# Attention with a null key and value: subtracting the null key, value and bias from the others

## The chip, the cores and the metric

The kernel runs on one core of a Trainium2 chip. The metric is the device time of one execution in microseconds (us). A core has five engines that run their own instruction streams in order and meet by semaphores: TensorE (PE; its weight loads are listed apart as PEld), VectorE (DVE), ScalarE (ACT), GpSimd (POOL) and SyncE (SP), which here issues nearly all transfers (DMAs).

## The reference

Multi-query attention with a null key, 64 sequences of 128 tokens, model width 512, 16 heads of width 64, one key and one value head for all of them. A layer norm comes before and after, and the input is added at the end.

```python
b, n, _ = x.shape                     # 64, 128
scale = DH ** (-0.5)
xn = layernorm(x, g_in)
q = (xn @ Wq).reshape(b, n, H, DH).transpose(0, 2, 1, 3) * scale
kv = xn @ Wkv
k, v = (kv[..., :DH], kv[..., DH:])
k = jnp.concatenate([nk, k], axis=1)  # nk = null_kv[0], the null key
v = jnp.concatenate([nv, v], axis=1)  # nv = null_kv[1], the null value
sim = jnp.einsum('bhid,bjd->bhij', q, k)
bias = jnp.concatenate([null_col, attn_bias], axis=-1)   # null_col: one number per head
sim = sim + bias
sim = jnp.where(causal_mask, neg, sim)
sim = jnp.where(mask_p[:, None, None, :], sim, neg)      # the null key is never masked
attn = jax.nn.softmax(sim, axis=-1)
out = jnp.einsum('bhij,bjd->bhid', attn, v)
out = out.transpose(0, 2, 1, 3).reshape(b, n, INNER) @ Wo
return x + layernorm(out, g_out)
```

Adding one number to all scores of a row leaves its softmax as it was. Since the weights of a row sum to one, the output is the null value plus the weighted sum of the values less the null value. Both kernels rest on the second fact; the second kernel also uses the first.

## The kernel before, in words

Everything is in 32-bit floats. A sequence is an item, four items are a group. One function, `step(n)`, runs from n = -6 to 62 and issues, in an order written out by hand, parts of the work of several items at once: statistics and normalisation of item n+10 or n+12, the token transposes, the query products of group (n+6)//4 (from the second group on by seven half-size products per block, `product`), keys and values of item n+6 (`kv_mm`, `kv_out`, `k_T`, `kT_out`), scores and softmax of items n+1 and n+2, weighted values of item n (`values`), and the output projection of items n-3 to n-1. All engines work through their streams in the order in which `step` wrote them.

**Keys, values and null scores.** `kv_mm` (L303) multiplies an item's 128 tokens by `wkv`, in four chunks of 128 rows of the model width; each call of the matmul is two PE instructions. `wkv` has 64 key columns, 64 value columns and 16 more, which give the null score of each head: the head's query weights times the null key, prepared before the steps by `weights_kv_prod` (POOL, a product over 1024 columns for each chunk) and `weights_kv` (VectorE: scaling, a reduction and `null_order`, two small copies). `kv_out` copies the keys twice side by side, and adds `vnb` to values and null scores: minus the null value, and the null biases. `nulls_move` (L326) puts the lower half of the keys' values, and the null scores of the heads that the other half of the partitions needs, into the tile `nv`, by two copies on ScalarE and two DMAs on SP, once for three items and once for one item in each group.

**Scores.** Partitions hold 64 query rows of two halves of the heads, and a row of the score tile S has a null column, 64 lower keys, 128 keys and a null column again, 194 in all, for 8 heads. On POOL, `bias_add` (L460) fills the 192 key columns with bias plus mask, and `null_copy` (L473) copies the null scores from `nv` to the two null columns. `scores_add` adds the matmul results, `scores_max` and `exps` (VectorE, ScalarE) go over keys with the null column, `scale` (POOL) multiplies the keys by one over the sum, `blocks_T` transposes 32x32 blocks on VectorE, and `blocks_move` sends them, by 14 DMAs on SP (L601), to the tile `aTb`, from which `value_mm` (L634) multiplies by the values.

**The start.** Loads are issued on SP in the order of the code: the first four items, `wq`, null key, `wkv`, then in `load_second` items 4 to 6, the second half of the biases (`load_bias(1)`), the mask, null bias and null value. A transfer into an item's buffer waits until PE has transposed the item before. `causal` (L195) masks the biases on POOL; `causal(1)` covers all partitions, so `load_bias(0)` comes after it. Between the steps -6 and -5, and -5 and -4, the code that prepares weights, mask values and bias stands; after step -5 come the statistics of item 6 and the three sums of query weights (`weight_sums`), and in step -4 the statistics of item 7.

```python
        if n == -6:
            for kc in range(1, KC):
                weights_kv_prod(kc)
            causal(1)
            load_bias(0)
            for kc in range(2):
                weights_kv(kc)
```

Of the kernel before, what the change touches and what calls it, by code (L numbers as in the profile page):

```python
# [17 lines left out]
def kernel(  # L18
# [70 lines left out]
    KVN = 2 * DH + H  # L89
# [60 lines left out]
    nkb = const.tile([P, DH], FP, name="nkb")  # L150
    nvb = const.tile([P, DH], FP, name="nvb")
    nv2 = const.tile([P, 1], FP, name="nv2")
    nbh = const.tile([P, H], FP, name="nbh")
    biasp = const.tile([P, R8, NL + N], FP, name="biasp")
# [13 lines left out]
    for kc in (3, 1):  # L168
        nc.sync.dma_start(out=wq[:, kc, :], in_=wq_r[:, kc, :])
    nc.sync.dma_start(out=nkb, in_=cond[0].partition_broadcast(P))  # L170
    nc.sync.dma_start(
        out=wkv[:, :, 0 : 2 * DH], in_=w_kv.rearrange("(kc p) f -> p kc f", p=P)
    )

    def load_second():
        for m in (4, 5, 6):
            load_x(m)
        load_bias(1)
        load_mask(0)
        nc.sync.dma_start(out=nbh, in_=null_bias.partition_broadcast(P))  # L180
        nc.sync.dma_start(out=nvb, in_=cond[1].partition_broadcast(P))
        for r in range(2):
            nc.sync.dma_start(
                out=nv2[r * DH : (r + 1) * DH, :], in_=cond[1].unsqueeze(1)
            )

    def load_bias(u):
        rows = slice(u * DH, (u + 1) * DH)
        bias_r = attn_bias.rearrange("(u f r) i j -> u r i f j", u=2, r=2)[u]
        for r in range(2):  # L190
            rf = slice(r * NF, (r + 1) * NF)
            nc.sync.dma_start(out=biasp[rows, rf, 0:NL], in_=bias_r[r, 0:DH, :, 0:NL])
            nc.sync.dma_start(out=biasp[rows, rf, NL:], in_=bias_r[r, DH:N])

    def causal(u):  # L195

        rows = slice(0, P if u else DH)
        for keys, base in ((slice(0, NL), -DH * u), (slice(NL, NL + N), DH - DH * u)):
# [9 lines left out]

    def load_late():
# [7 lines left out]
    nc.gpsimd.memset(biasp[0:DH], 0.0)  # L217

# [7 lines left out]
    vnb = const.tile([P, DH + H], FP, name="vnb")  # L226
# [7 lines left out]
    xT, qT, kT, vs, nv, mneg = {}, {}, {}, {}, {}, {}  # L234
# [66 lines left out]
    ktok = {}  # L301

# [13 lines left out]

    def kv_out(m, pkv):
        g, t = divmod(m, GB)
        k = bp.tile([P, 2, DH], FP, tag="ktok", name=f"ktok_{m}")
        nc.vector.tensor_copy(k, pkv[:, 0:DH].unsqueeze(1).broadcast_to([P, 2, DH]))  # L320
        ktok[m] = k
        if t == 0:
            vs[g] = hp.tile([P, GB, DH + H], FP, tag="vs", name=f"vs_{g}", bufs=3)
        nc.vector.tensor_tensor(vs[g][:, t, :], pkv[:, DH:], vnb, ALU.add)

    def nulls_move(g, ts):  # L326

        if ts.start == 0:
            nv[g] = hp.tile([P, GB, DH + H], FP, tag="nv", name=f"nv_{g}")
        lo, hi = slice(0, DH), slice(DH, P)  # L330
        n1, n0 = slice(DH, DH + R8), slice(DH + R8, DH + H)
        nc.scalar.copy(nv[g][lo, ts, n1], vs[g][lo, ts, n0])
        nc.scalar.copy(nv[g][hi, ts, n0], vs[g][hi, ts, n1])
        nc.sync.dma_start(
            out=nv[g][hi, ts, 0 : DH + R8], in_=vs[g][lo, ts, 0 : DH + R8]
        )
        nc.sync.dma_start(out=nv[g][lo, ts, n0], in_=vs[g][hi, ts, n0])
# [110 lines left out]
    def mask_neg(g):  # L448
        mneg[g] = gp.tile([P, GB, NL + N], FP, tag="mneg", name=f"mneg_{g}", bufs=1)
        m8 = m8s.pop(g).rearrange("p (t j) -> p t j", t=GB)  # L450
        for keys, m in ((slice(0, NL), m8[:, :, 0:NL]), (slice(NL, NL + N), m8)):
            nc.vector.tensor_scalar(
                mneg[g][:, :, keys], m, 0.0, NEG, ALU.is_equal, ALU.mult
# [6 lines left out]
    def bias_add(b):  # L460
# [3 lines left out]
        else:  # L464
            S[b] = sp.tile([P, R8, ROW], FP, tag="s", name=f"s_{b}")
        nc.gpsimd.tensor_tensor(  # L466
            S[b][:, :, 1 : ROW - 1],
            biasp,
            mneg[g][:, t].unsqueeze(1).broadcast_to([P, R8, NL + N]),
            ALU.add,  # L470
        )

    def null_copy(b):  # L473
        g, t = divmod(b, GB)
        nc.gpsimd.tensor_copy(
            S[b][:, :, 0 : ROW : ROW - 1],
            nv[g][:, t, DH:].rearrange("p (k e) -> p e k", k=2),
        )

# [154 lines left out]
    def value_mm(b, u, half, keys, vals, slots, start=True):  # L634
        for r in range(2):
            nc.tensor.matmul(  # L636
                pos[b][u][r * DH : (r + 1) * DH, half],
                vals[keys, b % GB, 0:DH],
# [8 lines left out]
    def values(b, split):  # L647
# [6 lines left out]
        g = b // GB  # L654
# [5 lines left out]
        value_mm(b, 0, 0, lo, vs[g], slice(0, 2))  # L660
        value_mm(b, 1, 0, hi, nv[g], slice(0, 2))
        if split:
            value_mm(b, 0, 1, lo, vs[g], slice(2, 4))
            value_mm(b, 1, 1, hi, vs[g], slice(4, 6))
# [4 lines left out]
        else:  # L669
            value_mm(b, 0, 1, slice(0, P), vs[g], slice(2, 4))  # L670
            value_mm(b, 1, 1, slice(0, P), vs[g], slice(4, 6))

    def values_end(b, split):
        g = b // GB
        if split:
            value_mm(b, 1, 1, lo, vs[g], slice(4, 6), start=False)
            value_mm(b, 0, 1, hi, vs[g], slice(2, 4), start=False)
# [174 lines left out]
    prods = {}  # L852

    def null_order(out, heads):

        for u in range(2):
            nc.vector.tensor_copy(
                out[:, (1 - u) * R8 : (2 - u) * R8].rearrange("p (r f) -> p r f", r=2),
                heads[:, u * R8 : (u + 1) * R8].rearrange("p (f r) -> p r f", r=2),
            )  # L860

    def weights_kv_prod(kc):

        pool, tag = ((sp, "s"), (sp, "s"), (hp, "sb"), (hp, "xb"))[kc]
        bufs = None if kc < 2 else 1
        prods[kc] = pool.tile([P, H, DH], FP, tag=tag, name=f"prod_{kc}", bufs=bufs)
        nc.gpsimd.tensor_tensor(
            prods[kc],
            wq[:, kc, :].rearrange("p (h d) -> p h d", d=DH),
            nkb.unsqueeze(1).broadcast_to([P, H, DH]),  # L870
            ALU.mult,
        )

    def weights_kv(kc):
        nc.vector.tensor_scalar(
            wkv[:, kc, 0 : 2 * DH], wkv[:, kc, 0 : 2 * DH], gin[:, kc : kc + 1], None, ALU.mult
        )
# [436 lines left out]
```

## Time and profile before

| what | before |
|---|---|
| three timed runs | 1120.65, 1121.5, 1123.69 us (median 1121.5) |
| span of the profiled execution | 1117.9 us |
| around the span: median less span | 3.6 us |
| PE, DVE, ACT, POOL busy in the span | 1088.6, 808.8, 676.5, 743.0 us |
| pk matmuls (L308), 128x144 | 488 of 286 ns |
| null copies (L475) | 64 of 205 ns |
| bias_add (L466) | 64 of 3455 ns |
| ktok copies (L320), 128 columns | 61 of 280 ns |
| vs additions (L324), 80 columns | 61 of 231 ns |
| copies of nulls on ACT (L332, L333) | 64 of 186 to 208 ns |

The page gives the span, from the first to the last instruction; of the whole profiled execution it gives no other time. A line of the profile names the source line, the engine, the operation, the tile written and the tiles read, the shape and the count; behind a bar stand the total busy time and the mean of one in ns, then the idle time of the engine just before and what ended it. In an order of time the columns are start and length in us. [...]

### The profile page before, as it was taken

How to read it: one execution, taken by the hardware profiler on the slowest of the kernel's cores; microseconds unless marked ns; L12 is line 12 of the kernel's file. 1: busy time of each engine (PE TensorE's matmuls, PEld its weight loads, DVE VectorE, ACT ScalarE, POOL GpSimd, SP SyncE). 2: the span in 40 equal slices, each digit the busy share in tenths (PEclk: the TensorE clock that was granted, in tenths of full speed). 3: DMA queues.
4: the chain of work that ended last, by engine and by line, in shares of the span. 5: the costliest groups of instructions: out<-in, count | busy, mean ns of one | idle time of the engine just before them, and what ended most of it. 6: DMA issues, size and time to landing. Idle time of an engine off the chain costs nothing.

```text
span 1117.9 us, 27535 instructions
## 1 busy us (share of the span) xinstructions
PE 1088.6 (97%) x9794; PEld 875.1 (78%) x9794; DVE 808.8 (72%) x1743; ACT 676.5 (61%) x2709; POOL 743.0 (66%) x587
## 2 busy tenths in 40 slices
PE   8899999999999999999999999999999999999987
PEld 6576788888888788888888888888888888888633
DVE  6576578777768767777877877877776786666862
ACT  2365577565667566667656667756666765657651
POOL 6446967577676667758566676757767675677832
PEclk9999999999999999999999999999999999999999
DMA  5323244443634534354343534444353453422333
GB/s 189 125 70 71 79 137 125 128 118 91 169 97 126 132 108 131 101 149 113 128 127 89 159 100 138 124 128 119 93 168 99 125 133 114 106 68 76 98 106 99
DMA packets 107864, 130.09 MB, mean 116 GB/s; under 512 B 29264, under 2 KB 72528, under 8 KB 105936
## 3 DMA queue, kind: packets, MB, share of 16 engines
q1 hardware_dynamic: 106480, 126.96, 40.1%
q8 instruction: 78, 1.28, 0.5%
q10 hardware_dynamic: 1248, 1.38, 0.4%
q14 instruction: 58, 0.48, 0.1%
HBM read 54.86 MB, written 31.46 MB: 77 GB/s over the span
## 4 chain that ended last, share of the span: by engine, by line
PE 70%; DVE 7%; DMA 7%; SPq 6%; POOL 4%; issue 3%; ACT 3%; POOLq 0%; DVEq 0%; ACTq 0%
PE pa L422 15%; PE pyX L750 14%; PE pyY L750 7%; PE ps L495 7%; PE po L636 7%; PE pc L422 7%; DMA x<-in_x_dram 6%; SPq L601 4%; PE pk L308 4%; PE pw L422 3%; PE pyw L750 3%; PE py L697 2%; ACT s L522 2%; POOL s L466 1%; SPq L295 1%
## 5 line engine op out<-in xcount | busy, mean ns | idle before, releaser
L522 ACT ACTIVATE s<-s,nmax 128x65 f32<-128x65 f32 (+1 forms) x1024 | 372.0, 368 | 0.4
L466 POOL TENSOR_TENSOR s<-biasp,mneg 128x1536 f32<-128x1536 f32 x64 | 221.1, 3455 | 101.4 <-DVE sb L575 98.2
L543 POOL TENSOR_TENSOR s<-s,rinv 128x512 f32<-128x512 f32 (+1 forms) x128 | 189.3, 1479 | 122.8 <-DVE nmro L794 89.8
L680 ACT ACTIVATE oT<-po,nv 128x512 f32<-128x512 f32 x128 | 80.9, 683 | 200.1 <-PE po L636 198.8
L522 ACT ACTIVATION_READ_ACCUMULATOR s<-s,nmax 128x1 f32 x1024 | 194.7, 190 | 0.0
L750 PE MATMUL pyX<-wT,oT 128*128 128x256 f32 x696 | 164.8, 380 | 0.5 <-DVE kyu L762 0.5
L750 PEld LDWEIGHTS pyX<-wT,oT 128*128 128x128 f32 x696 | 131.8, 190 | 19.7 <-DVE kyu L762 0.9
L495 PEld LDWEIGHTS ps<-kT,qT 64*64 64x64 f32 x4096 | 94.2, 133 | 45.4 <-DVE s L508 23.1
L508 DVE TENSOR_TENSOR s<-ps,s 128x512 f32<-128x512 f32 (+1 forms) x128 | 121.5, 949 | 8.1 <-PE ps L495 6.6
L422 PE MATMUL pa<-xS,wq 128*128 128x256 f32 x480 | 123.5, 380 | 1.0 <-ACT ku L433 1.0
L495 PE MATMUL ps<-kT,qT 64*64 64x64 f32 (+1 forms) x4096 | 118.0, 249 | 3.6 <-DVE s L508 2.7
L513 DVE TENSOR_REDUCE nmax<-s 128x8 f32<-128x520 f32 (+1 forms) x128 | 120.1, 939 | 1.5
L575 DVE STREAM_TRANSPOSE sb<-s 128x1536 f32<-128x1536 f32 x62 | 110.0, 1774 | 13.4 <-POOL s L543 6.5
L636 PE MATMUL po<-aTb,vs 64*64 64x256 f32 (+1 forms) x1240 | 119.1, 378 | 0.0
L433 ACT COPY ku<-pa 128x256 f32<-128x256 f32 x120 | 44.6, 372 | 88.4 <-PE pa L422 88.2
L422 PEld LDWEIGHTS pa<-xS,wq 128*128 128x128 f32 x480 | 86.7, 190 | 11.2 <-ACT ku L433 1.8
L308 PE MATMUL pk<-wkv,xT 128*128 128x144 f32 x488 | 69.9, 286 | 0.0
L422 PE MATMUL pa<-xS,wS 128*128 128x256 f32 x240 | 67.8, 405 | 0.0
L443 DVE TENSOR_TENSOR qT<-pw,kp 128x256 f32<-128x256 f32 x60 | 25.4, 424 | 56.9 <-ACT kp L433 56.9
L636 PEld LDWEIGHTS po<-aTb,vs 64*64 64x64 f32 (+1 forms) x1240 | 57.4, 133 | 10.2 <-issue 3.8
L308 PEld LDWEIGHTS pk<-wkv,xT 128*128 128x128 f32 x488 | 63.4, 191 | 0.1
L804 ACT ACTIVATE yn<-y,nmro,rstdo 128x512 f32<-128x512 f32 x58 | 45.3, 782 | 29.2 <-DVE nmro L794 29.2
(120 smaller groups left out, 2096.3 us busy)
## 6 DMA issues: line engine op xcount, KB each, us to landing
aTb<-sb SPq DMA_DIRECT2D x369, 64.0 KB
x<-in_x_dram SPq DMA_DIRECT2D x64, 256.0 KB
res<-in_x_dram SPq DMA_DIRECT2D x64, 256.0 KB
out_dram<-y SPq DMA_DIRECT2D x64, 256.0 KB
aTb<-sb SPq DMA_DIRECT2D x492, 32.0 KB
xd<-xb SPq DMA_DIRECT2D x14, 1024.0 KB
xT<-xd SPq DMA_DIRECT2D x56, 256.0 KB
wo<-in_L_cond_Wo_dram SPq DMA_DIRECT2D x1, 2048.0 KB
```

The lines of the kernel that those rows point to most:

```text
L308: nc.tensor.matmul(pkv, xT[g][:, t, kc, :], wkv[:, kc, :], start=(kc == 0), stop=(kc == KC - 1),)
L422: nc.tensor.matmul(prod[tag], w[:, kc, f * P : (f + 1) * P], t[:, :, kc, :], start=(start and kc == 0), stop=(kc == HK - 1), skip_group_ch ...
L466: nc.gpsimd.tensor_tensor(S[b][:, :, 1 : ROW - 1], biasp, mneg[g][:, t].unsqueeze(1).broadcast_to([P, R8, NL + N]), ALU.add,)
L495: nc.tensor.matmul(pv[u * DH : (u + 1) * DH, r, f, :], qT[g][rows, f, t, hf, u], kT[b][rows, 0:nk], start=True, stop=True,)
L508: nc.vector.tensor_tensor(sv, pss.pop((b, hf)), sv, ALU.add)
L513: nc.vector.tensor_reduce(nmax[b][:, hf], S[b][:, :, WITH_NULL[hf]], AX.X, ALU.max, negate=True)
L522: nc.scalar.activation(row, row, AF.Exp, bias=nmax[b][:, hf, k : k + 1], accum_out=rsum[b][:, hf, k : k + 1],)
L543: nc.gpsimd.tensor_tensor(sv, sv, rinvs.pop((b, hf)).unsqueeze(2).broadcast_to([P, R8, sv.shape[2]]), ALU.mult,)
L575: nc.vector.transpose(sb.rearrange("p j e q -> p e j q"), S[b][:, :, 1 : ROW - 1].rearrange("p e (j k) -> p e j k", k=Q),)
L636: nc.tensor.matmul(pos[b][u][r * DH : (r + 1) * DH, half], vals[keys, b % GB, 0:DH], aT_of(b)[keys, slots, r * NF : (r + 1) * NF], start=s ...
L680: nc.scalar.activation(oT[b][:, u * NF : (u + 1) * NF, :].rearrange("p f (s q) -> p s f q", q=Q), po[u].rearrange("p h i f q -> p (h i) f q"),
L750: nc.tensor.matmul(prod[key], h[:, c, :], w[:, c, :], start=(start and c == 0), stop=(c == HC - 1), skip_group_check=not start,)
```

## The change

Null key, null value and null bias are subtracted from the keys, the values and the biases; then the null score is zero for every row, and no column is computed, moved or copied for it.

- `wkv` keeps its 128 columns. The products, reductions and reordering that filled the other 16 go, and `weights_kv` is one multiplication over all four chunks.
- `kv_out` subtracts the null key and the null value, broadcast to all partitions in `nkv`, from keys and values.
- `nulls_move` becomes `values_move`, which is one DMA; the two ScalarE copies and the second DMA go.
- Bias and mask tiles get the null columns of S, filled once with zero, and `bias_add` covers all 194 columns of a row; `null_copy` goes. The mask tile is one fixed tile.
- `null_shift` subtracts each head's null bias from the biases on VectorE, after `causal(1)` and after `causal(0)`.

```diff
-    KVN = 2 * DH + H
+    KVN = 2 * DH
...
-    biasp = const.tile([P, R8, NL + N], FP, name="biasp")
+    biasp = const.tile([P, R8, ROW], FP, name="biasp")
...
-    nc.sync.dma_start(out=nkb, in_=cond[0].partition_broadcast(P))
-    nc.sync.dma_start(
-        out=wkv[:, :, 0 : 2 * DH], in_=w_kv.rearrange("(kc p) f -> p kc f", p=P)
-    )
+    nc.sync.dma_start(out=wkv, in_=w_kv.rearrange("(kc p) f -> p kc f", p=P))
...
+    def null_shift(u):
+
+        rows = slice(u * DH, (u + 1) * DH)
+        nc.vector.tensor_copy(
+            nbp[rows].rearrange("p (r f) -> p r f", r=2),
+            nbh[rows, u * R8 : (u + 1) * R8].rearrange("p (f r) -> p r f", r=2),
+        )
+        nc.vector.tensor_tensor(
+            biasp[rows, :, 1 : ROW - 1],
+            biasp[rows, :, 1 : ROW - 1],
+            nbp[rows].unsqueeze(2).broadcast_to([DH, R8, NL + N]),
+            ALU.subtract,
+        )
...
+    nc.gpsimd.memset(biasp[DH:, :, 0 : ROW : ROW - 1], 0.0)
...
+    nc.gpsimd.memset(mneg[:, :, 0 : ROW : ROW - 1], 0.0)
...
-        nc.vector.tensor_copy(k, pkv[:, 0:DH].unsqueeze(1).broadcast_to([P, 2, DH]))
+        nc.vector.tensor_tensor(
+            k,
+            pkv[:, 0:DH].unsqueeze(1).broadcast_to([P, 2, DH]),
+            nkv[:, 0:DH].unsqueeze(1).broadcast_to([P, 2, DH]),
+            ALU.subtract,
+        )
...
-        nc.vector.tensor_tensor(vs[g][:, t, :], pkv[:, DH:], vnb, ALU.add)
+        nc.vector.tensor_tensor(vs[g][:, t, :], pkv[:, DH:], nkv[:, DH:], ALU.subtract)
...
-        nc.scalar.copy(nv[g][lo, ts, n1], vs[g][lo, ts, n0])
-        nc.scalar.copy(nv[g][hi, ts, n0], vs[g][hi, ts, n1])
-        nc.sync.dma_start(
-            out=nv[g][hi, ts, 0 : DH + R8], in_=vs[g][lo, ts, 0 : DH + R8]
-        )
-        nc.sync.dma_start(out=nv[g][lo, ts, n0], in_=vs[g][hi, ts, n0])
+        nc.sync.dma_start(out=nv[g][hi, ts], in_=vs[g][lo, ts])
...
         nc.gpsimd.tensor_tensor(
-            S[b][:, :, 1 : ROW - 1],
+            S[b],
             biasp,
-            mneg[g][:, t].unsqueeze(1).broadcast_to([P, R8, NL + N]),
+            mneg[:, t].unsqueeze(1).broadcast_to([P, R8, ROW]),
             ALU.add,
         )
-
-    def null_copy(b):
...
-    def weights_kv(kc):
-        nc.vector.tensor_scalar(
-            wkv[:, kc, 0 : 2 * DH], wkv[:, kc, 0 : 2 * DH], gin[:, kc : kc + 1], None, ALU.mult
-        )
-        nq = small.tile([P, H], FP, tag="nq", name=f"nq_{kc}")
-        nc.vector.tensor_reduce(nq, prods.pop(kc), AX.X, ALU.add)
-        null_order(wkv[:, kc, 2 * DH :], nq)
+    def weights_kv():
+        nc.vector.tensor_tensor(
+            wkv, wkv, gin.unsqueeze(2).broadcast_to([P, KC, KVN]), ALU.mult
+        )
...
         if n == -6:
-            for kc in range(1, KC):
-                weights_kv_prod(kc)
             causal(1)
+            null_shift(1)
             load_bias(0)
-            for kc in range(2):
-                weights_kv(kc)
+            weights_kv()
         if n == -5:
-            for kc in range(2, KC):
-                weights_kv(kc)
             causal(0)
+            null_shift(0)
             mask_neg(0)
-            nc.vector.tensor_scalar(vnb[:, 0:DH], nvb, -1.0, None, ALU.mult)
-            null_order(vnb[:, DH:], nbh)
```

## The prediction

> **What bounds the kernel now.** I read the page first (busy shares, then the chain that ended last), then the busy time by stage, then the groups with shapes kept apart, then the order of time in the first 50 us and in one steady stretch on SyncE's queue.
>
> ```profile
> span 1117.9 us, 27535 instructions
> ...
> PE 1088.6 (97%) x9794; PEld 875.1 (78%) x9794; DVE 808.8 (72%) x1743; ACT 676.5 (61%) x2709; POOL 743.0 (66%) x587
> ...
> PE 70%; DVE 7%; DMA 7%; SPq 6%; POOL 4%; issue 3%; ACT 3%; POOLq 0%; DVEq 0%; ACTq 0%
> ```
>
> TensorE (PE) carries 70% of the chain; no other engine has 8%. By stage (columns: PE, weight load, DVE, ACT, POOL, granted clock, DMA share, GB/s):
>
> ```profile
> 20.00:46.00 26.00, 21.36 (x74) 12.14 (x73) 18.17 (x41) 6.58 (x11) 15.79 (x11) 0.93 0.41 125
> ...
> 100.00:130.00 30.00, 27.74 (x268) 21.90 (x261) 19.12 (x42) 19.82 (x83) 26.85 (x22) 1.00 0.24 62
> ...
> 330.00:530.00 200.00, 198.49 (x1842) 166.28 (x1841) 151.22 (x330) 127.68 (x511) 137.39 (x109) 1.00 0.44 123
> ```
>
> From 130 to 1040 us PE is busy over 99% (198.49 of 200 here), so a microsecond of its stream is about a microsecond of the span. Only before 130 us and after 1040 us does something else end waits. Two places matter. In 20 to 46 us PE idles 4.6 us and the clock falls to 0.93; the matmuls (PE) and the engines they wait for, in order of time (start, length, what):
>
> ```profile
> 36.00 0.60 PE L268 MATMUL pxT<-ident,x 128*128 128x128 f32 x4
> 36.43 1.15 PE L308 MATMUL pkv<-wkv,xT 128*128 128x144 f32 x8
> 41.44 2.19 PE L308 MATMUL pkv<-wkv,xT 128*128 128x144 f32 x8 [3.86 <-ACT xT L269]
> ...
> 44.25 1.58 PE L308 MATMUL pkv<-wkv,xT 128*128 128x144 f32 x8 [0.41 <-DVE vs L324]
> ...
> 32.02 0.69 DVE L241 BATCH_NORM_STATS2 st<-x 128x6 f32<-128x512 f32 x1
> ...
> 30.08 1.08 POOL L199 TENSOR_SCALAR_AFFINE_SELECT biasp<-biasp 64x1024 f32<-64x1024 f32 x1 [0.44 <-DMA biasp<-in_fside_16xSxS_dram]
> ```
>
> The 3.86 us is VectorE's lateness: statistics of x_6 at 32.02, three weight sums, statistics of x_7, then ScalarE's normalisation of x_7 at 39.61, and behind that in ScalarE's order the eviction of xT which pkv waits for. The second place is SyncE's queue at the start of every fourth step:
>
> ```profile
> 365.41 0.61 SPq L120 DMA_DIRECT2D x<-in_x_dram  x1
> 366.13 0.69 SPq L334 DMA_DIRECT2D nv<-vs  x1
> 366.86 0.64 SPq L337 DMA_DIRECT2D nv<-vs  x1
> 369.88 11.27 SPq L601 DMA_DIRECT2D aTb<-sb  x14
> ...
> SPq L601 <- DMA x<-in_x_dram: 18.0, 17, 2.1
> ```
>
> A train of 14 attention-block moves mostly takes 9.0 to 10.5 us (9.05 at 353.78); behind an x load with a late landing it takes 11.27 to 11.87, and there PE stalls at po: I count 0.59, 0.83, 1.46, 0.64, 0.41 and 0.67 us from the matmul starts, 4.6 us in all. In the built program the eight hardware DMA semaphores go round, so each transfer waits for the one eight places ahead.
>
> **The change, part by part.** Profiled span 1117.9; the timed median is 1121.5, so 3.6 us lie around the span, which I keep.
>
> 1. *K/V projection, 144 to 128 columns.* 488 pk matmuls are in this group:
>
> ```profile
> L308 PE MATMUL pk<-wkv,xT 128*128 128x144 f32 x488 | 69.9, 286 | 0.0
> ...
> 12.99 0.83 PE L1214 MATMUL busy<-ident 128*128 128x128 f32 x6
> ```
>
> A row of eight takes 1.15 us with 0.286 for the last, so starts are (1.15-0.286)/7 = 123 ns apart. For 128 columns, with a 128x128 weight load each, there are two rows: four transposes start at 36.00 and the next matmul at 36.43, 108 ns apart; six "busy" matmuls take 0.83 us with 0.275 for one, 111 ns apart. I take 110.5: 12.5 ns x 488 = **-6.1 us** (ends 12 and 15 ns: -5.9 and -7.3). The 24 pkv are in the startup stall and count there. [...]
>
> 2. *Queue places.* Two value moves become one (32 DMAs and about 0.6 us of issue each leave SyncE's queue). In the step above x now stands one place nearer the train, so the train's seventh move, not its sixth, waits for x, and one issue (11.27/14 = 0.8 with the wait, 0.6 without) no longer lies behind the landing. Of six stalls of 4.6 us, 0.6 x 6 = 3.6 at most goes (0.41 and 0.59 cannot give more than themselves); but their length is set off PE, so a PE that does two K/V groups less 0.1 us each grows them by 0.2 x 6 = 1.2. I take **-2.0** (ends 0.0 and -3.4; +1.2 if the place brings nothing). Next late is the following move's landing.
>
> 3. *Startup, VectorE and POOL.* Out go four POOL products (9.8 us), four reductions (4.8), four scalings (5.2) and ten small copies and one scaling (3.0). In come one scaling of 512 columns (0.7, as L809's 692 ns for that size), two copies (0.17 each) and two bias subtractions of 64x1536 (1.8 each: L387's 1.22 for 1024 and L575's 1774 ns for 1536). But the subtraction waits for the masked bias, and in VectorE's order it stands ahead of the mask, the statistics of x_6, the weight sums and the statistics of x_7. POOL, without products, masks the first half on landing (about 17.5 to 19 instead of 23.98); the loads of the second half no longer wait for it but for the x load ahead of them on SyncE (issued 21.47, held by PE's transposes), so they start at 21.84 instead of 24.67 and end 3.2 us earlier. The mask of 30.08 moves to 26.9, ends at 28.0, the subtraction ends at 29.8, mask values (0.55), statistics of x_6 at 30.35 instead of 32.02: **-1.65 us** of the 3.86 (the wait of DVE itself, about 4 us, costs nothing else: what stands behind it is counted here). Ends: loads land as late as before, then 30.08+1.08+1.8+0.55 = 33.5 against 32.02, +1.5; all of the wait goes, -3.9. I take -1.65 by the issue rows. One row warns: a wkv scaling took 2.23 us while POOL multiplied and 0.28 while it waited. At both subtractions POOL's next work waits for VectorE, so I charge nothing; if it bit, +2 us. [...] Two more memsets run at 1.3 to 5.6 us, where POOL idles 2.96; one broadcast load less at 4.66 lets wkv's load start earlier, while x_4 still waits for PE.
>
> 4. *Clock.* The two groups of eight after the stall take 2.19 and 1.58 us against 1.15 at full clock: 1.04 + 0.43 = 1.47 us of slow clock. The stage's 0.93 goes with a 3.86 us gap; gaps of 1.02 and 0.45 near 10 us left the clock at 1.00. Shrunk to 2.2 the gap lies between; ends 0 and -1.47, I take **-1.0**, nearer the short gaps. [...]
>
> 5. *POOL around 100 to 130 us*, where it is 26.85 of 30 busy and released PE's pyY at 125.24. Two of 64 null copies (13.1 us in all, 205 ns each) lie there: -0.4; bias_add grows from 1536 to 1552 columns, 3455 x 16/1536 = 36 ns, twice. **-0.35** (ends 0, -0.6). The other copies, and 27.5 us in which POOL waited for the value move, are covered by PE: POOL is 66% busy; likewise bias_add's 2.3 us more.
>
> 6. *K minus null key* costs VectorE nothing: copying 128 columns is 280 ns; a PSUM+SBUF subtraction is 231 for 80 columns and 416 for 256, so (416-231)/176 x 48 + 231 = 281. Values go from 80 to 64 columns, -17 ns. 64 ScalarE copies (12.6 us in all) are under PE's cover; without it at most one 0.4 us pair a step.
>
> Sum: -6.1 -2.0 -1.65 -1.0 -0.35 = -11.1; span 1106.8, with the 3.6 around it **1110.5 us**.
>
> **Rivals.**
> - *The startup gives nothing*: bias lands late, the subtraction (a new wait on VectorE) holds x_6 as long as the reductions did, +1.5, and the clock still drops. For it: the in-order wait, rows of 256 and 512 bytes at the same DMA rates. Against: 2.8 us earlier issue. -6.1-2.0-0.35+1.5 = 1114.5.
> - *Narrower matmuls don't pay*: loads of weights (191 ns each by their row) hold the spacing at 123. Against: 108 and 111 ns above. Then -5.0: 1116.5.
> - *PE's gain is given back*: the four-step cycle is a loop through x landing (9.6 us), SyncE and VectorE, and all 16 cycles, not six, pull even. 0.2 x 16 = 3.2 back, no queue gain, no startup gain: 1121.5-6.1+3.2-0.35+1.5 = 1119.8, within the noise.
> - *VectorE becomes the bound (slower)*: the key subtraction reads PSUM and a stride-0 SBUF operand and pays POOL's interference of 2 us (2.23-0.28) in each of 61 steps. VectorE has 16.4-12.4 = 4 us free a step, but kT, ktok and vs stand ahead of x's statistics, whose chain ends in the PE stalls. It decides once it costs over 0.18 us a step on that path (61 x 0.18 = 11). At 2 us in the 16 x-bound steps: +32-11 = 1142. Against: 231 ns for vs, of the same operand kinds beside a working POOL.
> - That the arithmetic is not removed can be left out: in the built program no instruction on null columns but the wider bias_add is left.
>
> **How the numbers follow.** Chances: forecast 0.66 (own range 1106 to 1113.5), startup nothing 0.14, narrow matmul 0.07, given back 0.07, slower 0.06. The measurement tells about 0.3%, 3.4 us: faster means under 1118.1. The first three cases are faster (0.87), given back is same (0.07), the last slower (0.06). The low end takes -7.3-3.4-3.9-1.47-0.6 = -16.7 reduced to 1106, since not all ends come together; the high end takes in the narrow-matmul case: 1117.
>
> **What would show it.** L308's spacing near 110 ns and its group's mean near 272; trains behind the x load about 0.6 us shorter and fewer po stalls; PE's wait before the second pkv near 2.2 us and 20 to 46 us at clock 1.00; ktok at 281 ns; POOL without its wait on nv. Wrong would be: ktok or the subtraction far above 0.3 and 1.8 us, a second pkv later than 41.4 us, or po stalls in most cycles.

## The result, and the profile after

The changed kernel takes 1106.85 us in the median of four runs (1106.42 to 1110.19); the kernel before took 1121.97 us beside it. The ratio is 0.988, with a 95% interval of 0.986 to 0.990: 1.2% faster. The prediction was 1110.5 us.

In the profiled execution, which took 1106.42 us, the span is 1104.5 us, so 1.9 us lie around the span (1.7 to 2.2 in all executions, of either kernel and of every experiment). The prediction kept 3.6 us there, which mixed the span of one execution with the median of others. Of the span itself 13.4 us went.

The page of the changed kernel, span, busy time and chain by engine:

```profile
span 1104.5 us, 27326 instructions
...
PE 1081.3 (98%) x9794; PEld 868.1 (79%) x9794; DVE 795.7 (72%) x1729; ACT 665.5 (60%) x2645; POOL 706.0 (64%) x521
...
PE 81%; DVE 5%; DMA 4%; ACT 4%; SPq 3%; POOL 2%; issue 1%; DVEq 0%; POOLq 0%; ACTq 0%
```

PE's share of the chain rose from 70% to 81%, DMA and SyncE's queue fell from 13% to 7%. The busy times by stage (columns: PE, weight load, DVE, ACT, POOL, granted clock, DMA share, GB/s):

```profile
20.00:46.00 26.00, 24.14 (x84) 12.79 (x83) 15.87 (x37) 6.92 (x12) 10.07 (x8) 1.00 0.39 113
100.00:130.00 30.00, 28.50 (x209) 23.09 (x208) 18.77 (x41) 18.63 (x80) 27.00 (x19) 1.00 0.31 78
330.00:530.00 200.00, 199.54 (x1857) 166.86 (x1856) 153.25 (x335) 126.84 (x506) 134.54 (x97) 1.00 0.44 122
```

PE idles 1.9 us from 20 to 46 us (4.6 before) and 0.46 us from 330 to 530 us (1.51 before). Both programs issue the same 9794 matmuls in the same order, so the start of matmul number k in the two traces says where the time went:

| matmul | before | after | gained so far |
|---|---|---|---|
| 400 | 75.75 | 72.64 | 3.1 |
| 1200 | 162.54 | 158.20 | 4.3 |
| 7200 | 812.42 | 801.05 | 11.4 |
| 8400 | 943.08 | 930.08 | 13.0 |
| last | 1111.69 | 1098.28 | 13.4 |

So in these two executions 3.1 us come from the startup, 1.2 from there to 160 us, 8.7 from the steady stage, 0.4 from the end. One execution is a coarse measure of a stage: from matmul 1200 to 8400 this one took 771.9 us, and that of an experiment below that changes only the startup (*The statistics of x_6 ahead of the subtraction*) took 775.8. A difference between two steady stages is good to about 4 us.

The groups that answer to those shown of before:

```profile
L321 PE MATMUL pk<-wkv,xT 128*128 128x128 f32 x488 | 64.5, 275 | 0.0
...
L335 DVE TENSOR_TENSOR ktok<-pk,nkv 128x128 f32<-128x128 f32 x61 | 17.1, 280 | 0.0
...
L479 POOL TENSOR_TENSOR s<-biasp,mneg 128x1552 f32<-128x1552 f32 x64 | 205.3, 3208 | 112.0 <-DVE sb L580 108.8
```

A row of eight pk matmuls now takes 1.06 us with 0.275 for the last, so starts are 112 ns apart against 123: each starts before the one ahead of it has ended, and in a row one costs the spacing. The key subtraction takes the 280 ns of the old copy. bias_add covers 16 columns more and takes 247 ns less, which the prediction did not expect. In order of time, SyncE's queue ahead of a train of the changed kernel:

```profile
423.54 0.62 SPq L120 DMA_DIRECT2D x<-in_x_dram  x1
424.26 0.53 SPq L351 DMA_DIRECT2D nv<-vs  x1
427.91 10.31 SPq L606 DMA_DIRECT2D aTb<-sb  x14
```

And from its waits (us in total, times, longest), SyncE's for x and PE's for the moved blocks:

```profile
SPq L606 <- DMA x<-in_x_dram: 9.6, 11, 1.5
...
PE po L641 <- DMA aTb<-sb: 1.3, 1, 1.3
```

The trains behind the four xT loads take 10.49 us in the mean of the twelve between 130 and 930 us (9.77 to 11.10) against 11.22; behind anything else the means are 9.3 to 9.6 in both kernels. SyncE waits 9.6 us for x in 11 moves, not 18.0 us in 17. PE waits 1.3 us for moved blocks, not 4.3, but 3.0 of the 4.3 and all of the 1.3 lie after 1040 us; for the steady stage the matmul starts say more. Counted from them, between 130 and 930 us, the six gaps at po of 0.41 to 1.46 us (4.6 in all) are gone, and three of 0.17 to 0.29 (0.65 in all) are left. Four of 0.34 to 0.39 have come up at ps, the scores, where PE waits for VectorE and not for a move (three of the four in one line, with lengths from the modelled ends of 130 to 930 us):

```profile
PE ps L500 <- DVE done L673: 0.7, 3, 0.2
```

The startup of the changed kernel, PE and VectorE in order of time:

```profile
37.40 1.06 PE L321 MATMUL pkv<-wkv,xT 128*128 128x128 f32 x8
40.00 1.13 PE L321 MATMUL pkv<-wkv,xT 128*128 128x128 f32 x8 [1.55 <-DVE vs L344]
41.44 0.33 PE L356 MATMUL pkT<-ident,ktok 128*128 128x128 f32 x1 [0.31 <-ACT xT L284]
41.73 1.13 PE L321 MATMUL pkv<-wkv,xT 128*128 128x128 f32 x8
42.70 0.27 PE L356 MATMUL pkT<-ident,ktok 128*128 128x128 f32 x1
42.81 1.45 PE L387 MATMUL pq<-xT,wq 128*128 128x512 f32 x3
...
29.81 1.75 DVE L215 TENSOR_TENSOR biasp<-biasp,nbp 64x1536 f32<-64x1536 f32 x1 [4.20 <-POOL biasp L198]
31.48 0.61 DVE L465 TENSOR_SCALAR mneg<-m 128x256 f32<-128x256 uint8 x2
32.02 0.68 DVE L256 BATCH_NORM_STATS2 st<-x 128x6 f32<-128x512 f32 x1
```

In this execution the statistics of x_6 start at 32.02, exactly as before. Yet the second pkv starts at 40.00 instead of 41.44, because it now waits for VectorE's vs and not for ScalarE's eviction of xT (40.80 to 41.39 in both profiles): as built, it writes the PSUM buffer that the first pkv left, not the one that the transposes left. The eviction now delays only the later pkT, by 0.31 us, and the groups after it run at 1.13 us, at full clock.

The start at 32.02 belongs to this execution, in which the clock was halved from 11.93 to 15.34 us. Four experiments below keep the startup order of the changed kernel (the width undone, the value move split by partitions, POOL's wait, bias_add in rows), and in their profiles the clock is full there. The statistics of x_6 then start at 29.98 to 30.39 us and the second pkv at 37.96 to 38.38. From the one with the split move, VectorE and PE:

```profile
28.07 1.75 DVE L215 TENSOR_TENSOR biasp<-biasp,nbp 64x1536 f32<-64x1536 f32 x1 [2.96 <-POOL biasp L198]
...
30.28 0.68 DVE L256 BATCH_NORM_STATS2 st<-x 128x6 f32<-128x512 f32 x1
...
38.26 1.13 PE L321 MATMUL pkv<-wkv,xT 128*128 128x128 f32 x8 [1.33 <-DVE vs L344]
```

### The profile page after: what moved, and what is told of

It reads as the page before. It is cut to its first block, busy times and chain, and to the rows that moved or that the text cites. A ratio compares the mean times of both kernels' runs of the same rounds, so it can differ in the third digit from the quotient of the medians.

```text
span 1104.5 us, 27326 instructions
## 1 busy us (share of the span) xinstructions
PE 1081.3 (98%) x9794; PEld 868.1 (79%) x9794; DVE 795.7 (72%) x1729; ACT 665.5 (60%) x2645; POOL 706.0 (64%) x521
## 4 chain that ended last, share of the span: by engine, by line
PE 81%; DVE 5%; DMA 4%; ACT 4%; SPq 3%; POOL 2%; issue 1%; DVEq 0%; POOLq 0%; ACTq 0%
PE pa L436 17%; PE pyX L755 16%; PE pc L436 8%; PE pyY L755 8%; PE ps L500 8%; PE po L641 7%; PE pk L321 4%; PE pw L436 4%; PE pyw L755 4%; DMA x<-in_x_dram 3%; PE py L702 3%; ACT s L527 2%; SPq L606 2%; PE pq L387 1%; DVE s L513 1%
## 5 line engine op out<-in xcount | busy, mean ns | idle before, releaser
L479 POOL TENSOR_TENSOR s<-biasp,mneg 128x1552 f32<-128x1552 f32 x64 | 205.3, 3208 | 112.0 <-DVE sb L580 108.8
L641 PE MATMUL po<-aTb,vs 64*64 64x256 f32 (+1 forms) x1240 | 115.3, 379 | 0.0
L261 POOL TENSOR_TENSOR rstd<-rstd,nhalf 128x1 f32<-128x1 f32 x64 | 35.7, 558 | 60.4 <-DVE rstd L260 55.4
L321 PE MATMUL pk<-wkv,xT 128*128 128x128 f32 x488 | 64.5, 275 | 0.0
```

Source lines behind the costliest of these rows:

```text
L321: nc.tensor.matmul(pkv, xT[g][:, t, kc, :], wkv[:, kc, :], start=(kc == 0), stop=(kc == KC - 1),)
L479: nc.gpsimd.tensor_tensor(S[b], biasp, mneg[:, t].unsqueeze(1).broadcast_to([P, R8, ROW]), ALU.add,)
L641: nc.tensor.matmul(pos[b][u][r * DH : (r + 1) * DH, half], vals[keys], aT_of(b)[keys, slots, r * NF : (r + 1) * NF], start=start, stop=Tru ...
```

## The experiments

All times stand beside runs of the kernel before on the same chip. A ratio is to that kernel; differences between two experiments are good to about 3 us, as their intervals say.

### The width alone, undone and done

The changed kernel with the old width (16 columns of zeros):

```diff
-    KVN = 2 * DH
+    KVN = 2 * DH + H
...
+    nc.gpsimd.memset(wkv[:, :, 2 * DH :], 0.0)
```

> The changed kernel with the K/V projection 144 columns wide again (16 zero columns in the weights, results not used), nothing else. My theory: the pk matmuls start 123 ns apart again instead of 112, 488 x 11.5 ns = 5.6 us more, 1106.9 -> 1112.5 us, nearly all of it between 130 and 1030 us. Rival (the gain came from POOL and SyncE, the projection's width was covered): no more than 1 us, below 1108.

Measured: 1109.62 us, ratio 0.9894 (0.9876 to 0.9912). That is 2.8 us more than the changed kernel by the medians, 1.6 with 3.1 either way by the ratios, where the longer spacing alone is 488 x 11 ns = 5.4 us. Its pk matmuls stand 123 ns apart again (69.9 us in the group, as before the change), but SyncE waits less for x than in the changed kernel, and the gaps at po and ps, 2.2 us in sum there, are 0.6 us here:

```profile
SPq L609 <- DMA x<-in_x_dram: 5.8, 11, 1.0
```

That fits a loop in which a slower PE gives x more time to land.

The other direction, the kernel before with its projection narrowed. It leaves out the products of the queries with the null key. All else is kept but for VectorE: the addition of the values is narrowed too, and a copy per group puts in the null biases.

```diff
-                pkv,
+                pkv[:, 0 : 2 * DH],
...
-                wkv[:, kc, :],
+                wkv[:, kc, 0 : 2 * DH],
...
+            nc.vector.tensor_copy(
+                vs[g][:, :, DH:], vnb[:, DH:].unsqueeze(1).broadcast_to([P, GB, H])
+            )
```

> The kernel before with the K/V projection narrowed to 128 columns and nothing else changed: the 16 null columns of the moving tile are not multiplied (this leaves out the products of the queries with the null key: the null scores hold only the null bias), all copies, both null moves and every wait stay. Theory (PE and SyncE's train share the four-step cycle, so part of what PE saves comes back as longer po stalls, as the widened kernel showed with 2.8 us of 5.6): spacing 111 ns, the K/V part 5.4 us shorter, the po stalls longer than the 4.6 us of before, in all 2 to 3.5 us faster than before, about 1119. Rival of the prediction's sum (every nanosecond of PE's stream counts): 5.4 to 6.1 us faster, about 1116.3. Rival that the cycle is wholly SyncE's: no change, 1122.

Measured: 1118.85 us, ratio 0.9965 (0.9953 to 0.9978): 3.3 us by the medians, 2.5 to 5.3 by the ratio. The waits of this kernel (in total, times, longest):

```profile
SPq L606 <- DMA x<-in_x_dram: 21.0, 17, 2.6
...
PE po L641 <- DMA aTb<-sb: 6.0, 6, 1.7
```

Before they were 18.0 us and 4.3 us; the trains behind the x load grew from 11.22 to 11.41, and the gaps at po between 130 and 930 us from 4.6 to 6.5. So about 2 us of the 5.4 came back as longer waits, with spacing at 112 ns as it should be. That PE's own loop alone lengthened them is not shown, since this run also has the copies on VectorE:

```profile
L324 DVE COPY vs<-vnb 128x64 f32<-128x64 f32 x16 | 9.3, 580 | 0.0
```

The changed kernel has no such copies, and there the width is worth at most 4.7 us by the ratios. Both runs say that the narrowing pays less than its own length, neither by much more than its uncertainty.

### The queue place alone, undone and done

First the changed kernel with its value move split by columns into two:

```diff
-        nc.sync.dma_start(out=nv[g][hi, ts], in_=vs[g][lo, ts])
+        for c in (slice(0, 48), slice(48, DH)):
+            nc.sync.dma_start(out=nv[g][hi, ts, c], in_=vs[g][lo, ts, c])
```

> The changed kernel with each move of the values split into two DMAs of 48 and 16 columns, so that SyncE's queue has as many transfers as before. My theory: in the step behind each x load the train's sixth move waits for x again, those trains take 11.3 us and more instead of 10.2 to 10.8, and the po stalls come back: 2 to 3.4 us more, 1109 to 1110.3. Rival (stalls came from elsewhere): no change, 1106.9, with trains as long as in the changed kernel.

Measured: 1114.89 us, ratio 0.9945 (0.9926 to 0.9964), 8.0 us more than the changed kernel by the medians, 7.3 with 3.2 either way by the ratios, over twice what was expected of the place. Trains behind the x load took 11.75 us. But the split also doubled the number of row pieces, so a second split was made by partitions, with as many rows and bytes as the one move:

```diff
-        nc.sync.dma_start(out=nv[g][hi, ts], in_=vs[g][lo, ts])
+        for r in (slice(0, Q), slice(Q, DH)):
+            d = slice(DH + r.start, DH + r.stop)
+            nc.sync.dma_start(out=nv[g][d, ts], in_=vs[g][r, ts])
```

> The changed kernel with its one value move split by partitions into two DMAs of 32 rows: as many rows of the same bytes as in one move, one more place on SyncE's queue, no other work. If the queue place made the 8 us that the split by columns cost: trains behind the x load near 11.8 us, po stalls in most cycles, about 1115. If the smaller pieces made them (the split by columns doubled the pieces): 1107 to 1108. Both: between, and the distance tells the shares.

Measured: 1114.35 us, ratio 0.9933 (0.9916 to 0.9949): 7.5 us more than the changed kernel by the medians, 5.9 with 3.0 either way by the ratios. So it is the place that costs, and the pieces add nothing that can be told from it. SyncE's queue and one po of this kernel in order of time:

```profile
426.93 0.61 SPq L120 DMA_DIRECT2D x<-in_x_dram  x1
427.64 1.21 SPq L353 DMA_DIRECT2D nv<-vs  x2
431.11 11.06 SPq L608 DMA_DIRECT2D aTb<-sb  x14
...
378.15 0.43 PE L643 MATMUL po<-aTb,nv 64*64 64x256 f32 x2 [1.46 <-DMA aTb<-sb]
```

Its waits:

```profile
SPq L608 <- DMA x<-in_x_dram: 24.9, 18, 2.3
...
PE po L643 <- DMA aTb<-sb: 6.0, 7, 1.5
```

One transfer of 0.6 us between x and the train makes the trains 1.0 us longer (11.53 against 10.49), and PE waits at po in most cycles (nine gaps of 0.37 to 1.62 us). In the steady stage (matmul 1200 to 8400) its profiled execution is 9.0 us longer than the changed kernel's.

Then the kernel before with one of its two moves taken off SyncE:

```diff
-        nc.scalar.copy(nv[g][lo, ts, n1], vs[g][lo, ts, n0])
+        nc.scalar.copy(nv[g][lo, ts, DH:], vs[g][lo, ts, DH:])
...
-        nc.sync.dma_start(out=nv[g][lo, ts, n0], in_=vs[g][hi, ts, n0])
```

> The kernel before with one of its two null moves (that of the lower half's null columns) replaced by a ScalarE copy within the same partitions, so the lower half's null scores are those of other heads: one DMA less a cycle stage on SyncE's queue, PE's work unchanged. Theory that the queue places are worth much more than the 2.0 us of the prediction (putting the second move back into the changed kernel cost 8): the trains behind the x load fall from 11.15 to about 10.5 us, the po stalls of 4.6 us go almost wholly, 4 to 6 us faster, about 1117. The prediction's step: 2.0 us faster, 1120. Rival (the 8 us came from the smaller pieces of that split, not from the place): no change, 1122.

Measured: 1117.11 us, ratio 0.9952 (0.9936 to 0.9968), 5.1 us less than the kernel before (3.6 to 7.2 by the ratio). Its waits:

```profile
SPq L600 <- DMA x<-in_x_dram: 8.8, 10, 1.4
...
PE po L635 <- DMA aTb<-sb: 1.4, 2, 1.2
```

The trains fell from 11.22 to 10.55 us, the gaps at po between 130 and 930 us from 4.6 to 0.8 us, and the steady stage of the profiled execution became 4.4 us shorter with PE's work unchanged. So the place is worth about all of the 4.6 us that the prediction counted as stalls, not the 2.0 us it took.

### Where x stands in the queue

If the place of x sets the train, x can be moved. Ahead of the four xT loads:

```diff
+        if n < B3:
+            transfers()
         if (n + 8) % GB == 0 and 2 <= (n + 8) // GB < NG:
             tokens_in((n + 8) // GB)
-        if n < B3:
-            transfers()
```

> The changed kernel with the res and x loads issued ahead of the four xT loads in every fourth step: x is issued 2.0 us earlier, the xT loads 1.1 us later, nothing else. Theory (the train behind x still waits for x's landing, 9.6 us in 11 of 16 cycles, and this sets the train's end and with it PE's po): that wait goes, the trains fall from 10.5 to about 9.5 us, the last po waits on the moves go; the stalls left are small, so 1 to 3 us faster, 1104 to 1106. Rival (PE is the bound now, over 99% busy): no change, 1107. Against both: the xT loads land later and xS or kT is late, slower by up to 1.1 us in 14 cycles, 1115 or more.

Measured: 1118.81 us, ratio 0.9972 (0.9954 to 0.9990): 12 us slower than the changed kernel by the medians, 10.3 with 3.1 either way by the ratios. The theory forgot its own mechanism; the expectation's second rival named the time (1115 or more). Each transfer waits for the one eight places ahead (in the changed kernel's trace SyncE's transfers take eight semaphores in turn, 147 to 150 transfers each); x is issued 2 us earlier but stands six places before the train instead of two, so the train's third move waits for it, and the next four wait for the xT loads. The waits say so:

```profile
SPq L606 <- DMA xT<-xd: 19.7, 39, 1.1
SPq L606 <- DMA x<-in_x_dram: 14.5, 10, 2.5
...
PE po L641 <- DMA aTb<-sb: 13.4, 11, 2.1
```

39 waits for xT are four in each of some ten trains, as four places give. That rival's own reason, xT late for PE, is seen too but smaller: 2.8 us of waits at pw, which reads xT.

One place nearer the train, behind the value move:

```diff
+        if n % GB or n <= 0:
+            loads_x(n)
...
             values_move((n + 3) // GB, slice(0, GB - 1))
+            if n > 1:
+                loads_x(n - 1)
```

> The changed kernel with the x load of every fourth step issued behind the value move and not ahead of it: one place nearer the train, so the train's eighth move, not its seventh, waits for x's landing; x is issued at most 0.7 us later. Theory (a place is 0.7 us of issue against x's landing of 9.6 us, and the loop through it still ends some waits: SyncE 9.6 us behind x in 11 cycles, four po gaps of 0.34 to 0.39 us): trains behind x load about 10.0 instead of 10.5 us, 0.5 to 1.5 us faster than the changed kernel, 1105.5 to 1106.5. Rival (PE is the only bound now): 1107. Rival (x issued later costs what the place gives): 1107, with trains at 10.5.

Measured: 1109.65 us, ratio 0.9885 (0.9868 to 0.9902), not to be told from the changed kernel's 0.988. The trains did shorten, to 10.19 us, and SyncE waits 3.7 us for x in 6 moves, not 9.6 in 11; one train:

```profile
422.26 0.51 SPq L355 DMA_DIRECT2D nv<-vs  x1
422.81 0.61 SPq L120 DMA_DIRECT2D x<-in_x_dram  x1
426.58 9.70 SPq L610 DMA_DIRECT2D aTb<-sb  x14
```

The mechanism is again right, and no gain is seen within 3 us: the changed kernel has only 0.65 us of gaps at po left to win in its steady stage.

Last, x behind the train:

```diff
+        if n % GB or n <= 0:
+            loads_x(n)
...
         if eb in sbs:
             blocks_move(eb)
+        if n % GB == 1 and n > 1:
+            loads_x(n - 1)
```

> The changed kernel with the x load of every fourth step issued behind the train, so no move of the train waits for it: theory, the trains behind the four xT loads fall from 10.5 to 9.1 to 9.6 us, SyncE's waits for x (9.6 us) are gone, no po gap over 0.3 us is left between 130 and 930 us; PE is then the only bound there: 1 to 2.5 us faster, 1104.5 to 1106. Rival: x comes 13 us later and its statistics or the transposes wait, or the xT landing takes x's part in the train: 1107 or slower.

Measured: 1233.45 us, ratio 1.0993 (1.0969 to 1.1018). The trains fell to 9.77 us, near the 9.1 to 9.6 expected, but the statistics of x stand in VectorE's order right there: the rival came, at a far larger price. VectorE and PE in one cycle, in order of time:

```profile
410.65 0.69 DVE L260 BATCH_NORM_STATS2 st<-x 128x6 f32<-128x512 f32 x1 [10.92 <-DMA x<-in_x_dram]
...
413.66 2.07 PE L440 MATMUL pc<-xS,wS 128*128 128x256 f32 x4 [7.99 <-POOL xS L422]
```

The granted clock of the stretch (seventh column behind the bounds), PE's wait in total, and its busy time on the page:

```profile
410.22:417.05 6.83, 3.39 (x40) 2.33 (x40) 4.89 (x14) 3.12 (x12) 4.57 (x5) 0.50 0.18 58
```

```profile
PE pc L440 <- POOL xS L422: 96.0, 12, 8.8
```

```profile
PE 1112.1 (90%) x9794; PEld 881.6 (72%) x9794; DVE 796.8 (65%) x1729; ACT 665.2 (54%) x2645; POOL 705.8 (57%) x521
```

VectorE waits 10.92 us for x, POOL's power and sums stand behind that, and PE stops for 8 us until POOL has the sums, while the clock halves around each of twelve stops. PE's wait of 96.0 us and 31 us more busy time by the halved clock (1112.1 against 1081.3) make 127, which is the difference to the changed kernel.

The same with the wide projection was to show what the width is worth without the loop through x:

> The kernel with the x load behind the train, and with the 144-column projection put back as in the widened kernel. Theory (half of the narrowing came back only because PE ran into SyncE's loop through x): without that loop the width costs its whole 488 x 11.2 ns = 5.5 us, so this is 4.5 to 6 us slower than the one with x behind the train and 128 columns. Rival (the loop is elsewhere, or the narrowing is worth 2.8 us for another reason): 2 to 3.3 us slower.

Measured: 1237.61 us, ratio 1.1026 (1.1008 to 1.1044), 4.2 us more by the medians and 3.7 with 3.4 either way by the ratios. This tells nothing: the value lies between both expectations, and the ground of the test, a PE without the loop, was not reached.

### POOL's wait and bias_add

The changed kernel with a small POOL subtraction that waits for the moved values, as null_copy did:

```diff
+    def null_zero(b):
+        g, t = divmod(b, GB)
+        v = nv[g][DH:, t, 0 : 2 * R8].rearrange("p (k e) -> p e k", k=2)
+        nc.gpsimd.tensor_tensor(S[b][DH:, :, 0 : ROW : ROW - 1], v, v, ALU.subtract)
```

> The changed kernel with one small POOL subtraction an item (64 partitions x 16, the moved values less themselves, into the null columns) where the null copy stood, so that POOL waits for the move of the values again. My theory: POOL gets its 64 x 0.2 us and some 20 to 27 us of waits back, and PE covers them: 1106.9, at most 0.5 more from around 100 to 130 us. Rival (the null copies and their wait on POOL carried a large part of the gain): 3 us and more, 1110.

Measured: 1110.09 us, ratio 0.9893 (0.9873 to 0.9912): 3.2 us more by the medians, 1.5 with 3.2 either way by the ratios. The wait is back in full, 27.0 us of POOL's idle time:

```profile
L491 POOL TENSOR_TENSOR s<-nv 64x16 f32<-64x16 f32 x64 | 13.8, 216 | 32.7 <-DMA nv<-vs 27.0 <-DVE vs L344 1.7
```

Whether it costs nothing or some 3 us is inconclusive.

bias_add over 192 columns of each row again, with the null columns of S set by a memset:

```diff
-            S[b],
-            biasp,
-            mneg[:, t].unsqueeze(1).broadcast_to([P, R8, ROW]),
+            S[b][:, :, 1 : ROW - 1],
+            biasp[:, :, 1 : ROW - 1],
+            mneg[:, t, 1 : ROW - 1].unsqueeze(1).broadcast_to([P, R8, NL + N]),
...
+        nc.gpsimd.memset(S[b][:, :, 0 : ROW : ROW - 1], 0.0)
```

> The changed kernel with POOL's bias_add over 192 of 194 columns of each row again (as before the change), the two null columns of the scores set to zero by a memset. Theory (the whole-tile shape, read and written without gaps, is why bias_add fell from 3455 to 3208 ns although it has 16 columns more): bias_add at 3.45 us again, POOL's busy time up by 16 us and the memset; the time within 1 us of the changed kernel, 1106 to 1108, since POOL's work lies beside PE's. Rival (the 247 ns came from a quieter memory, one DMA and 16 POOL copies less a cycle): bias_add stays near 3.2 us. Rival on time: POOL is on the path in 100 to 130 us and at the end: up to 1.5 us slower.

Measured: 1110.23 us, ratio 0.9885 (0.9867 to 0.9903), the same as the changed kernel. Its group on POOL:

```profile
L479 POOL TENSOR_TENSOR s<-biasp,mneg 128x1536 f32<-128x1536 f32 x64 | 204.0, 3187 | 108.4 <-DVE sb L581 105.2 <-DVE mneg L465 2.8 <-PE paL L621 0.4
```

The theory that reading the tile without gaps makes bias_add faster falls: in rows it takes 3187 ns. Every instance takes nearly the same (3.42 to 3.47 us before, 3.17 to 3.21 here), which speaks against a neighbour's traffic too. What still differs from the kernel before is the row pitch of the bias and mask tiles (194 columns, not 192) and the place of the tiles; that was not tried apart.

### The statistics of x_6 ahead of the subtraction

```diff
             causal(0)
-            null_shift(0)
-            mask_neg(0)
 
             norm_stats(6)
             norm_apply(6)
             weight_sums()
+            null_shift(0)
+            mask_neg(0)
```

> The changed kernel with the second bias subtraction and the first mask values put behind the weight sums in VectorE's order, so that the statistics of x_6 and the sums don't wait for the bias load. My theory: statistics of x_6 start near 26 to 28 us instead of 32.0, the second pkv about 1 us earlier than 40.0 us, and all later work moves with it: 1105.8. Rival (later waits of the start give it back): 1106.9.

Measured: 1107.46 us, ratio 0.9874 (0.9856 to 0.9892): no gain that can be seen. Its matmuls around the stall:

```profile
38.35 1.16 PE L321 MATMUL pkv<-wkv,xT 128*128 128x128 f32 x8 [1.64 <-ACT xT L284]
...
40.11 2.02 PE L321 MATMUL pkv<-wkv,xT 128*128 128x128 f32 x8 [0.50 <-DVE vs L344]
...
42.14 2.16 PE L387 MATMUL pq<-xT,wq 128*128 128x512 f32 x3
```

The statistics of x_6 start at 24.67 and the next ones at 34.48, 3.1 us earlier than in the changed kernel's profile and 1.0 to 1.5 us earlier than in the four profiles with a full clock at 12 us. But here the second pkv takes the buffer of the transposes and waits for ScalarE again, 1.6 us, and starts at 38.35, no earlier than the 37.96 to 38.38 of those four. What the statistics gain is lost again to the order of buffers. The clock halves in this execution too (2.02 us for the third pkv).

## Why the prediction was right or wrong

**Direction and size.** The forecast case came: faster, 1106.85 us against 1110.5, inside the case's own range (1106 to 1113.5). Of the 3.65 us missed, 1.7 are the term *around the span* (3.6 kept, 1.9 measured): the profiled execution of before was that much shorter than the median it stood beside. Measured by the medians the kernel gained 15.1 us where the terms add up to 11.1. That the total came so near is partly luck, since the width was priced too high and the queue place too low.

**1. Width: size of the instruction right, its worth too high.** The spacing is 112 ns in each kernel with 128 columns, where 110.5 was taken from the transposes; gross that is 488 x 11 = 5.4 us against 6.1. The step that failed is "a microsecond of its stream is about a microsecond of the span": narrowing alone is worth 2.5 to 5.3 us in the kernel before, and undoing it costs at most 4.7 by the ratios. The mechanism that fits is the third rival's, that PE runs into the loop through x's landing; the prediction gave it 1.2 us within the queue term and a chance of 0.07 for all of it, and about 2 us came back. This is argued from the longer waits and not shown, since the run in the kernel before also has 16 more copies on VectorE.

**2. Queue places: mechanism right, the term mis-sized.** The trains shortened by 0.73 us (11.22 to 10.49), where "about 0.6 us shorter" was said. The failed step is "0.6 x 6 = 3.6 at most goes": alone the place is worth 5.1 us (3.6 to 7.2), of 4.6 us of gaps at po 0.8 are left, and the gap of 1.46 us went as a whole; undone in the changed kernel it costs 7.5 (5.9 with 3.0 either way by the ratios). The cap of one issue per stall did not hold. A reading that fits is that a late train is not a cost of its own cycle alone, since PE, x's issue and the next train follow each other in a loop.

Whether the two terms add is not shown. In the profiled executions the place is worth 4.4 us of the steady stage with the wide PE and 9.0 with the narrow one, but the same steady code differs by 3.9 us between two profiles, and in whole times the two worths (5.4 with 1.8 either way, 5.9 with 3.0) can't be told apart.

**3. Startup on VectorE: mechanism right, a second gain not seen.** Predicted were bias loads issued at 21.84 and 1.65 us from statistics of x_6 at 30.35. In the four profiles with this startup and a full clock at 12 us the loads are issued at 21.55 to 21.98 and the statistics start at 29.98 to 30.39. In the changed kernel's own profile they start at 32.02, because the clock had fallen at 11.93 us: PE's transposes were late, the x load ahead of the bias loads went at 23.01 (21.12 to 21.55 in those four), and the bias loads at 23.45. One profile alone would have said that the mechanism had failed.

The second gain is the PSUM buffer of the second pkv, which the prediction did not look at although the built program has it. In each of the four profiles the second pkv starts 1.4 us before the eviction of xT, which it had waited for before the change, has ended. By matmul 400 they are 3.2 to 4.6 us ahead of before (3.1 in the changed kernel's own profile) against 2.65 for this term and the clock together. That the buffer alone makes those 1.4 us was read from the traces and the built program, and not tested by itself. (What the prediction calls the statistics of x_7, and the description of the start places in step -4, are those of item 8; item 7's come later.)

**4. Clock: right in this execution, and a matter of chance.** 20 to 46 us ran at clock 1.00 instead of 0.93. But the clock fell for 3.41 us near 12 us, which no step foresaw:

```profile
11.93:15.34 3.41, 3.41 (x17) 3.41 (x17) 3.20 (x6) 1.36 (x3) 0.14 (x1) 0.50 0.81 244
```

Of the eleven profiles of kernels with the changed startup, two have such a fall near 12 us, three one near 40 us, about where before has it, and six none before 60 us. With the same startup order, matmul 400 starts at 72.57 us with a fall near 40 us and at 71.16 to 71.56 without: one fall costs 1.0 to 1.4 us, as the term said.

**5. POOL.** The null copies' share of 0.35 us can't be told apart; bias_add got faster by 247 ns, not slower by 36. **6.** The key subtraction at 280 ns against 281 expected, and the value subtraction at 213 against 214, so the rival of a slower VectorE found nothing.

**What stays open.** The kernel before with one move and the changed kernel with the wide projection share queue and width, and still differ by 7.5 us (6.5 with 2.7 either way by the ratios). The startup explains about 4 of them (4.2 by matmul 400 of these two profiles). The rest, 2 to 3 us and within the uncertainty, would come from the rest of the change, which the prediction costed at nothing: POOL's wait for the moved values, the ScalarE copies, the shorter bias_add. The run with POOL's wait put back points that way, within its uncertainty; it was not settled.

## What to carry to other kernels

When the chain shows two engines in turn in a steady loop, here PE and SyncE's train behind a load, don't price an edit by the length of its own instructions or issues alone: do it alone in the old kernel, undo it alone in the new one, and watch the waits of both engines. Before moving or adding a transfer, count the places between a late-landing load and the transfers that PE waits for; one small transfer there cost 6 to 8 us, more than all the columns taken from PE. Before issuing a load later, look where its first reader stands in an in-order stream: with x behind the train, VectorE waited 10.92 us for it in one cycle. And before explaining a startup or a stage from one profile, look at a second execution with the same code in that stage.

## What was not expected of the hardware

When the clock falls could be read more sharply than the prediction had it. In all traces the half-clock stretches begin on a grid of 3.413 us counted from the first change of the clock (before at 41.58 and 1116.78 us, 10 and 325 windows from 7.45; in the changed kernel at 11.93, 1056.41 and 1104.19, 2, 308 and 322 windows from 5.10), and last one, two or three such windows (the last is cut off by the end). The table counts the windows of this grid that ran at full clock, in all fourteen traces, by the time in them in which no matmul ran (from the starts and the modelled ends):

| PE idle within one window | windows | half clock in the next |
|---|---|---|
| under 1.0 us | 4402 | 0 |
| 1.0 to 1.6 us | 66 | 1 |
| 1.6 to 2.05 us | 18 | 8 |
| 2.05 to 3.4 us | 24 | 24 |
| the whole window | 27 | 27 |

So in these traces 2.05 us of idle time within a window were followed by half clock every time (51 of 51 windows, 24 of them not idle throughout), 1.6 to 2.05 us in 8 of 18, for a reason that the traces do not show, and less than 1.6 us in 1 of 4468. It need not be one gap: the fall at 11.93 us followed gaps of 1.41 and 0.83 us in one window.

The mask values over 256 columns (L452 before, L465 after) went from 1266 to 911 ns in the mean, at the same count and type. The layout of the tiles is not the cause: the run with POOL's wait put back has the layout of the changed kernel and 1249 ns. In all fourteen traces each of these 16 instructions either takes 0.24 to 0.29 us or ends 0.15 us after POOL's multiplication `s<-s,rinv` beside it has ended (145 to 154 ns, whether it took 0.56 us until then or 1.66). So where the two met in these traces, this VectorE instruction ended only behind that POOL instruction, and its mean tells only how much of the multiplication was left when it started. The change of bias_add (3455 to 3208 ns) is not explained by this.
